# One job of fifteen block products in place of two jobs of seven, in a fused graph-attention kernel

## The chip, the cores and the metric

The kernel runs on one core of a Trainium2 chip. The metric is the device time in microseconds (us). A profiled execution gives, besides, a trace of every instruction. The engines are called as in the profile: PE (TensorE, matrix products), PEld (its weight loads), DVE (VectorE), ACT (ScalarE), POOL (GpSimd) and SP (the queue that issues the DMAs). Each engine works through its own instructions in the order in which the program lists them.

## The reference, cut to what matters

Two graph-attention layers, each with a residual and a layer norm, on x of 128 graphs x 64 nodes x 768 features, all in float32. The change lies wholly in layer 0, which has 12 heads of 64:

```python
h = jnp.einsum('bnd,ade->bane', feat_in, W)
th = jnp.tanh(h)
attn = (th . w_src) + swapaxes(th . w_dst)          # per head
attn = jnp.where(attn >= 0, attn, 0.2 * attn)
attn = softmax(jnp.where(~adj, -999.0, attn))
feat_out = elu(attn @ h + b)
gate = jax.nn.sigmoid(feat_in @ H_w.T + H_b)
x = layernorm(x + gate * feat_out + (1.0 - gate) * feat_in)
```

Layer 1 is a masked attention with 6 heads of 128 (q, k, v, output projection). It follows as a second stage and the change leaves its arithmetic alone.

## The kernel before, in words

The 8192 nodes are 32 pairs of two tiles; a tile is 128 nodes (two graphs), so a pair is 256 rows. Stage 1 runs layer 0 and the v projection of layer 1, pair by pair; stage 2 runs q, k, attention and the output projection of layer 1.

In stage 1, h = x W (768 x 768) and the gate logits = x H (768 x 768) are each a product of a pair's 256 x 768 rows with a 768 x 768 matrix. Each is computed as a 2 x 2 block product in seven products instead of eight (class Job, L247): the x blocks are 128 rows x 384, the weight blocks 384 x 384, and sums of blocks replace the eighth product. A product is three matmuls of 384 columns (L270), one for each 128 of the 384 that are summed over. Four sums of x blocks per pair are made on POOL (L240 to L243, `block_sums`), four sums of weight blocks once on DVE (L216 to L219). The results leave PSUM as copies on ACT (L850, L852) and as adds on DVE (L851 for h, L866 to L868 for the gate, where the first write also adds the bias). The v projection (`v_job`, L871) has the same form.

The order on each engine is written out by hand. A list gives the order of PE's products in a turn (TURN: h1, h2, u4, u3, h6, g1, h5, h7, g2, ..., where h and g are of the new pair p, v of the old pair q = p - 1, and u is the rest of the v job before that). After the product at each position of the list, the actions planned for that position are emitted (`at` for the new pair, `was` for the old one). A product's way out of PSUM is emitted one product later (`step`, L305). PSUM banks are shared out by tag (y, z: three each, m: two).

For each tile of the new pair the actions are, in this order: `products` (tanh of h on ACT, L888, then times w_dst on DVE, L889, and w_src on POOL, L890), `terms` (L893: the sums over each head on DVE, L897; these 12 numbers per node go out to DRAM, L899, and come back spread over all partitions, L902, as the tile dd), `logits` (dd plus the own term, DVE, L926), `leaky` (ACT, L936), `masked` (mask, maximum, subtraction: DVE, L942, L948, L949), `exps` (ACT, L955). In the turn after, the tile is old: `probs_by_nodes` (transposes on PE, L966, copies on ACT, L967), `gate_tanh` (ACT, L1067, L1068), `residual` (POOL, L1017), `attend` (48 small matmuls, L987), `features` (DVE, L1003, L1004, then exp on ACT, L1011), `elu1` and `gated` (DVE, L1022, L1027, L1029), `stats` and `normed` (DVE, POOL L322, ACT L327), `by_features` (transposes and copies), and then the v products and their block sums (`v_sums`, DVE). The two tiles of the new pair are called n1 and n0 (n1 goes first), those of the old pair t1 and t0.

In TURN `terms` of n1 and n0 stand at positions 13 and 14, `logits` at 16 and 18, `masked` at 18 and 20, so that DVE's list reads: sums over heads of n1, two gate adds, sums of n0, two v block sums and a v add, logits of n1, and so on. Of PE's list around the turn's start: h1, transposes, h2, u4, attend of t1, u3, transposes, h6; the product that needs h1's way out of PSUM (h6) stands after `attend`.

Stage 2 uses the same idea with 15 products of 256 x 256 blocks (WIDE, classes Wide and Out, L447 and L494).

## Time and profile before

| what | value |
|---|---|
| three runs | 2884.24, 2886.47, 2887.24 us (median 2886.47) |
| span of the profiled execution | 2888.2 us (the page gives no other time for it) |
| stage 1, to the first key product of stage 2 | 1525.6 us |
| time from pair to pair in stage 1 (e.g. `features` of t1, 700.96 to 746.53) | 45.57 us |
| mean of that over 28 pairs (h1 at 140.97 to h1 at 1423.92) | 45.8 us |
| in that stretch of 45.57 us, busy: PE, DVE, POOL, ACT | 44.99, 37.12, 21.38, 20.02 us |
| granted PE clock, mean | 0.998 |

The busy time of an engine is the time in which at least one of its instructions ran; an idle entry in brackets behind an instruction gives how long the engine stood before it and what ended that. The "critical chain" is followed back from the last instruction to what released it, step by step.

### The profile page before, as it was taken

What the parts mean: (1) busy time and instruction counts of PE and PEld (TensorE: products, weight loads), DVE (VectorE), ACT (ScalarE), POOL (GpSimd) and SP (SyncE); (2) the same over time, 40 slices, a digit from 0 to 9 for tenths busy, and PEclk for the clock granted to TensorE, in tenths of its full rate; (3) what the DMA queues carried; (4) which work ended last, traced back from release to release, by engine and by line L of the source; (5) the groups of instructions that cost most, each with busy time, mean ns of one, the idle gap of its engine ahead of it and who ended that gap; (6) DMA issues with size and microseconds to landing.
All of it is one profiled execution on the core that took longest, in us unless ns stands there. A gap on an engine that the chain in (4) does not pass through costs nothing.

```text
span 2888.2 us, 47874 instructions
## 1 busy us (share of the span) xinstructions
PE 2840.2 (98%) x18252; PEld 2075.9 (72%) x18252; DVE 1924.9 (67%) x3203; ACT 1061.2 (37%) x1896; POOL 1303.5 (45%) x1253
## 2 busy tenths in 40 slices
PE   8999999999999999999999999999999999999998
PEld 4565556666566666666668888888888888888886
DVE  7888888887888888777763545555544555554556
ACT  2444444444444444444433223333222333322332
POOL 3444445454444544343343445343545443444534
PEclk9999999999999999999999999999999999999999
DMA  5444444444445444333353434432323333233432
GB/s 182 132 154 145 140 150 143 159 148 151 141 142 162 135 155 142 105 116 108 121 195 96 122 91 111 111 92 84 77 79 111 111 104 95 68 84 94 111 88 74
DMA packets 322068, 348.73 MB, mean 121 GB/s; under 512 B 147888, under 2 KB 247216, under 8 KB 321840
## 3 DMA queue, kind: packets, MB, share of 16 engines
q1 hardware_dynamic: 321840, 345.66, 39.7%
q8 instruction: 146, 2.39, 0.4%
q14 instruction: 82, 0.67, 0.1%
HBM read 198.48 MB, written 122.29 MB: 111 GB/s over the span
## 4 chain that ended last, share of the span: by engine, by line
PE 80%; DVE 9%; DMA 4%; ACT 3%; issue 2%; POOL 1%; SPq 1%; POOLq 0%; DVEq 0%; ACTq 0%
PE z_k L447 9%; PE z_o L494 9%; PE z_q L447 8%; PE y_h L270 6%; PE y_g L270 6%; PE y_k L447 6%; PE y_o L494 6%; PE y_q L447 5%; PE y_v L270 5%; PE z_h L270 4%; PE z_v L270 3%; PE z_g L270 2%; PE cp L634 2%; PE sp L550 2%; PE x_g L270 2%
## 5 line engine op out<-in xcount | busy, mean ns | idle before, releaser
L574 ACT ACTIVATE sc<-sc 128x512 f32<-128x512 f32 x48 | 30.7, 639 | 616.9 <-DVE sc L571 616.9
L695 POOL TENSOR_TENSOR y<-y,bf_bc 128x768 f32<-128x768 f32 x64 | 114.7, 1817 | 295.1 <-DMA y<-x1d 265.5
L507 DVE TENSOR_TENSOR y<-y,z_o 128x256 f32<-128x256 f32 x320 | 127.4, 417 | 140.0 <-PE z_o L494 139.9
L494 PE MATMUL z_o<-wf,so 128*128 128x256 f32 x896 | 215.8, 383 | 2.3 <-DVE y L507 1.2
L447 PE MATMUL z_q<-xs,w_wq 128*128 128x256 f32 x896 | 213.5, 381 | 1.0 <-POOL xs L411 0.9
L411 POOL TENSOR_TENSOR so<-ctxT 128x256 f32<-128x256 f32 x224 | 160.5, 737 | 89.8 <-PE y_o L494 44.0
L447 PE MATMUL z_k<-xs,hw_wk 128*128 128x256 f32 x840 | 200.0, 381 | 0.0
L447 PEld LDWEIGHTS z_q<-xs,w_wq 128*128 128x128 f32 x896 | 168.7, 190 | 25.0 <-POOL xs L411 1.3
L494 PEld LDWEIGHTS z_o<-wf,so 128*128 128x128 f32 x896 | 167.2, 190 | 26.9 <-issue 2.0
L322 POOL TENSOR_TENSOR rs_b<-ve_b,minus_half 128x1 f32<-128x1 f32 x64 | 40.5, 632 | 312.7 <-DVE ve_b L320 311.9
L1017 POOL TENSOR_TENSOR x<-gate,x 128x768 f32<-128x768 f32 x64 | 120.1, 1878 | 135.1 <-ACT gate L1068 121.6
L890 POOL TENSOR_TENSOR th<-th,wsd 128x768 f32<-128x768 f32 x64 | 118.0, 1844 | 137.7 <-DVE th L889 137.7
L447 PEld LDWEIGHTS z_k<-xs,hw_wk 128*128 128x128 f32 x840 | 160.3, 191 | 22.1
L322 POOL TENSOR_TENSOR rs_a<-ve_a,minus_half 128x1 f32<-128x1 f32 x64 | 35.9, 562 | 307.3 <-DVE ve_a L320 307.3
L411 POOL TENSOR_TENSOR xs<-r,r 128x512 f32<-128x512 f32 x112 | 147.8, 1338 | 39.5 <-DMA r<-x1Td 22.5
L462 DVE TENSOR_TENSOR qT<-qT,z_q 128x512 f32<-128x512 f32 x96 | 65.9, 687 | 140.8 <-PE z_q L447 140.8
L270 PE MATMUL y_h<-w_wq,xT 128*128 128x384 f32 x384 | 136.5, 492 | 8.3 <-DMA w_wq<-in_w_dram 7.7
L462 DVE TENSOR_TENSOR kT<-kT,z_k 128x512 f32<-128x512 f32 x96 | 66.0, 687 | 114.9 <-PE z_k L447 112.9
L270 PE MATMUL z_v<-wv,sv_v 128*128 128x384 f32 x384 | 137.5, 494 | 1.0 <-DVE v L880 1.0
L270 PE MATMUL y_v<-wv,x1T 128*128 128x384 f32 x384 | 136.5, 492 | 1.2 <-ACT v L879 0.9
L270 PE MATMUL z_h<-w_wq,sx_x 128*128 128x384 f32 x384 | 137.5, 494 | 0.0
L270 PE MATMUL y_v<-wv,sv_v 128*128 128x384 f32 x384 | 134.9, 488 | 1.9 <-DVE sv_v L241 1.0
(165 smaller groups left out, 6907.7 us busy)
## 6 DMA issues: line engine op xcount, KB each, us to landing
x<-in_x_dram SPq DMA_DIRECT2D x64, 384.0 KB, 3.7
dd<-dstd SPq DMA_DIRECT2D x128, 192.0 KB, 3.4
x1d<-x SPq DMA_DIRECT2D x64, 384.0 KB, 2.6
x1Td<-x1T SPq DMA_DIRECT2D x32, 768.0 KB, 4.5
vd<-v SPq DMA_DIRECT2D x64, 384.0 KB, 2.9
r<-x1Td SPq DMA_DIRECT2D x96, 256.0 KB, 3.4
v<-vd SPq DMA_DIRECT2D x384, 64.0 KB, 2.3
y<-x1d SPq DMA_DIRECT2D x64, 384.0 KB, 5.7
```

Of the source, the lines that this page charges most:

```text
L270: T.matmul(to[:, : self.n], lhsT, rhs, start=kc == 0 and not more, stop=kc == HK - 1, skip_group_check=more,)
L322: G.tensor_tensor(rstd, ve, minus_half, ALU.pow)
L411: G.tensor_tensor(t, self.of(x[0]), self.of(x[2]), x[1])
L447: T.matmul(b[:, half * W2 : (half + 1) * W2], w[:, kc, half * P : (half + 1) * P], x[:, kc, :], start=half == kc == 0 and not more, stop=k ...
L462: V.tensor_tensor(at, at, b.rearrange("p (h t) -> p h t", h=2), ALU.add if sign > 0 else ALU.subtract,)
L494: T.matmul(b[:, :W2], x[:, kc, :], w[:, kc, :], start=kc == 0 and not more, stop=kc == 1, skip_group_check=more,)
L507: V.tensor_tensor(at, at, self.banks[path][:, :W2], ALU.add if sign > 0 else ALU.subtract)
L550: T.matmul(self.sp_[gr * N : (gr + 1) * N, (i * 2 + a) * N : (i * 2 + a + 1) * N], qT[:, 2 * self.f + a, at], kT[:, 2 * self.f + a, at], s ...
L634: T.matmul(self.cp_[a][e, at], self.v_[rows, i, gr, e], self.scT_[rows, at], start=True, stop=True,)
L695: G.tensor_tensor(y, y, pools["bf"], ALU.add)
L890: G.tensor_tensor(th[:, 1, :], th[:, 1, :], wsd[:, 1, :], ALU.mult)
L1017: G.tensor_tensor(xp, st[t]["gate"], xp, ALU.mult)
```

## The change

- h and gate become one product: the 256 x 768 rows times one 768 x 1536 matrix (W and H side by side). It is cut 3 x 2 x 3: x blocks of 128 rows x 256, weight blocks of 256 x 512, in 15 products (PRODUCTS) instead of 18. Each product is two matmuls of 512 columns. The products run in the order ORDER, adding up in five paths; a path is one PSUM bank, and a product that adds to a path waits until the path's earlier readers have read.
- The weight blocks: nine are loaded, 17 sums (128 x 1024 numbers each) are made once on DVE (`made`) and one negation on ACT. Ten sums of x blocks per pair (128 x 256) on POOL take the place of four (128 x 384).
- Way out of PSUM per pair: six copies on ACT and ten adds on DVE, each 128 x 512, where there were four copies on ACT and ten operations on DVE, each 128 x 384. The gate's bias is added by POOL (`gate_bias`, two per pair, 128 x 768). h and gate of a tile lie in one tile hg, four of them in rotation.
- The turn's list becomes a0 a5 a3 a1 a8 a6 a7 a2 a10 a9 a12 a4 a14 a11 v1 v2 v6 v5 v7 a13 v4 v3; all seven v products are of the old pair. The actions move with it (below). For the first three pairs one stream of 45 products runs, with v of pairs 0 and 1 put in near its end.
- The weights of q and k of stage 2 go into the room of the new weight tile, in the order in which the last pair sets it free.

```diff
+PRODUCTS = [
+    (0, (2, 0), [(2, 0, -1)]),
+    (3, (1, 1), [(0, 1, -1)]),
...
+    (0, (2, ALU.add, (0, 0)), [(2, 1, -1)]),
...
+    (4, ((0, 1), ALU.subtract, 3), [(0, 1, 1), (1, 1, 1)]),
...
+ORDER = (0, 5, 3, 1, 8, 6, 7, 2, 10, 9, 12, 4, 14, 11, 13)
...
+HEAD = [f"a{n}" for n in ORDER[:14]]
+TURN = HEAD + ["v1", "v2", "v6", "v5", "v7", "a13", "v4", "v3"]
...
+        def negated():
+            S.mul(wa[:, 0], wa[:, 14], -1.0)
+
+        def made(i):
+            dst, a, op, b = MADE[i]
+            V.tensor_tensor(wa[:, dst], wa[:, a], wa[:, b], op)
...
+        class Fifteen:
...
+            def product(self, n):
+                path = PRODUCTS[n][0]
+                more = path in self.banks
+                if not more:
+                    tag = "y" if path in (0, 2) else "z"
+                    self.banks[path] = bank(tag, f"{tag}_a{self.p}_{n}", 3)
+                b, x = self.banks[path], A[self.p][n]
+                for kc in range(2):
+                    T.matmul(
+                        b,
+                        x[:, kc, :],
+                        wa[:, n, kc, :],
...
+            def way_out(self, n):
+                path, _, reads = PRODUCTS[n]
+                b = as_heads(self.banks[path])
+                for f, t, sign in reads:
...
+                    if (f, t) in self.written:
+                        V.tensor_tensor(at, at, b, ALU.add if sign > 0 else ALU.subtract)
+                    elif sign > 0:
+                        S.copy(at, b)
+                    else:
+                        S.mul(at, b, -1.0)
...
+        def gate_bias(t):
+            gt = gate_of(t)
+            G.tensor_tensor(gt, gt, as_heads(hb_bc), ALU.add)
...
+        stream = [(p, f"a{n}") for p in range(3) for n in ORDER]
...
+        for q, a0, a1 in ((0, 0, 36), (1, 37, 3 * NW - 1)):
+            items += stream[a0:a1] + values[q][:5] + stream[a1 : a1 + 1] + values[q][5:]
...
+                was(0, do(probs_by_nodes, t1), do(exps, t0), do(gate_tanh, t1))
+                was(1, do(residual, t1))
+                was(2, do(attend, t1), do(gate_tanh, t0))
+                was(3, do(features, t1), do(probs_by_nodes, t0), do(residual, t0))
...
+                was(11, do(v_begins, q), do(v_sum, q, 0), do(by_features, t0))
+                was(14, do(v_sum, q, 1), do(spill_features, q))
+                was(15, do(v_sum, q, 2))
+                was(17, do(v_sum, q, 3))
...
-            at(11, new, do(products, n1))
...
-            at(12, new, do(products, n0))
-            at(13, new, do(terms, n1), do(with_bias, n1))
-            at(14, new, do(terms, n0), do(with_bias, n0))
...
-            at(16, new, do(logits, n1))
-            at(17, new, do(leaky, n1))
...
-            at(18, new, do(masked, n1), do(logits, n0))
-            at(19, new, do(exps, n1), do(leaky, n0))
-            at(20, new, do(masked, n0))
+            at(7, do(products, n1))
+            at(8 if p != 1 else 15, do(inputs, p))
+            at(9, do(terms, n1), do(with_bias, n1))
+            at(12, do(logits, n1))
+            at(13, do(leaky, n1), do(products, n0))
+            at(14, do(masked, n1))
+            at(14 if p != 1 else 17, do(plus_one, p))
+            at(15, do(exps, n1), do(terms, n0), do(with_bias, n0), do(gate_bias, n0))
+            late = p == NP - 1
+            at(18 - late, do(logits, n0))
+            at(19 - late, do(leaky, n0))
+            at(20 - late, do(masked, n0))
+            at(21 if p < NP - 1 else 17, do(gate_bias, n1))
```

As the built program has it, DVE's list of a turn in the steady part becomes: features of t1; add of a1; elu1 and gated of t1; add of a8; stats of t1; add of a6; features of t0; mask; add of a7; elu1 and gated of t0; times w_dst of n1; stats of t0; add of a10; sums over heads of n1; add of a12; v block sum 1; add of a4; logits of n1; add of a14; times w_dst of n0; add of a11; v block sum 2; masked of n1; v block sum 3; sums over heads of n0; a v add; v block sum 4; logits of n0; a v add; add of a13; masked of n0; a v add. On ACT the negated copy of a0 stands behind exps of t0 and gate_tanh of t1; on PE, a3 (same path as a0) stands ahead of attend of t1.

## The prediction

> **What bounds the kernel now.** I read the page's busy times first, then PE's waits by stretch, then the critical chain and DVE's and PE's timelines of one pair.

> ```profile
> PE 2840.2 (98%) x18252; PEld 2075.9 (72%) x18252; DVE 1924.9 (67%) x3203; ACT 1061.2 (37%) x1896; POOL 1303.5 (45%) x1253
> ```

> PE is busy 98%; in the waits view it loses only 6.2 us between 200 and 1350 us. So stage 1 goes at PE's pace: 14 h and gate products, 7 of v, four sets of transposes and two `attend` per pair.

> ```profile
> 736.26 2.10 PE L270 MATMUL y_v<-wv,sv_v 128*128 128x384 f32 x6
> 738.20 2.10 PE L270 MATMUL y_h<-w_wq,xT 128*128 128x384 f32 x6
> ```

> Starts are 1.94 us apart (the 2.10 overlaps the next). 21 x 1.94 + 4 x 0.66 + 2 x 0.86 + 0.4 us of handing over = 45.5; one pair measured 45.57. But a second loop is almost as long. The critical chain, 724 to 747 us:

> ```profile
> 724.82 1.95 PE y_v L270 x6
> 726.77 0.36 SPq L902
> 727.17 3.83 DMA dd<-dstd
> 731.10 1.53 DVE att L926
> ...
> 743.20 0.84 ACT prob L955
> 744.04 0.74 ACT gate L1067
> 744.81 0.84 ACT gate L1068
> 745.65 0.38 ACT h L850
> 746.06 0.56 DVE h L851
> ```

> It leaves PE for a trip through DRAM (dd), goes through DVE and ACT, and returns to `features`. DVE's timeline of the same stretch:

> ```profile
> 723.38 1.74 DVE L897 TENSOR_REDUCE sd<-th 128x24 f32<-128x1536 f32 x1
> 725.04 0.54 DVE L866 TENSOR_TENSOR gate<-y_g,hb_bc 128x384 f32<-128x384 f32 x1
> ...
> 726.09 1.74 DVE L897 TENSOR_REDUCE sd<-th 128x24 f32<-128x1536 f32 x1
> 727.75 1.77 DVE L241 TENSOR_TENSOR sv_v<-sv_v,x1T 128x384 f32<-128x384 f32 x1
> ...
> 731.10 1.52 DVE L926 TENSOR_TENSOR att<-dd,sd 128x768 f32<-128x768 f32 x1 [0.65 <-DMA dd<-dstd]
> ```

> The sums over heads of n1 end at 725.12, dd is there at 731.10: the trip takes 6.0 us. DVE fills it with the gate adds, the sums of n0 and v block sums, and waits 0.65 us. This filling is what the change takes away.

> [...] at 746.06 DVE's add of h waits 2.47 us for ACT, and `features` behind it waits too. [...] Here six passes took 4.21 us, not 1.94, shortly after an idle stretch of 3.31 us:

> ```profile
> 82.86 1.54 PE L966 MATMUL x1Tp<-ident,x 128*128 128x128 f32 x6 [3.31 <-ACT x L327]
> 84.69 4.21 PE L270 MATMUL y_v<-wv,x1T 128*128 128x384 f32 x6 [0.29 <-ACT x1T L967]
> ```

> [...] Here L1022 takes 0.96 us alone and 1.35 to 1.85 beside POOL, while adds from PSUM keep their 0.55.

> **PE's part.** No 128x512 matmul is in stage 1, but a stage 2 product streams the same 2048 columns (8 passes of 256; the new one 4 of 512) and takes 1.73 us in the chain. 15 x 1.73 = 25.95 against 14 x 1.94 = 27.16: 1.2 us less, PE's pace 44.3 us per pair. With fewer, longer passes it may be 1.71 (0.3 us more gained). This counts only if PE stays the bound.

> **DVE's part.** Ten operations of 0.55 go; ten of 128x512 come. That shape from PSUM is on the page:

> ```profile
> L462 DVE TENSOR_TENSOR qT<-qT,z_q 128x512 f32<-128x512 f32 x96 | 65.9, 687 | 140.8 <-PE z_q L447 140.8
> ```

> 0.69 us each, in sequence about 0.6 (0.46 for the 0.55 one): +1.4 us per pair on 37.1. That alone would fit. The order does not. I add up the new loop from the start of `features` t1, in DVE's order, with spacings from 700.96 to 746.53:
> - features 1.4; add 0.6; wait for exp 0.4; elu1 and gated of t1 3.9 (as beside POOL before); add 0.6; stats 1.4; add 0.6; features t0 1.4; mask 0.3; add 0.6; elu1 and gated t0 3.1; w_dst of n1 1.0; stats 1.4; add 0.6; shift 0.5 (POOL's power now queues behind its 1.8 us multiply); sums of n1 1.7. Sum 19.5.
> - dd of n1: 6.0, now covered by only an add, a v sum and an add (1.7): DVE stands 4.3. Behind this wait are queued the adds of a14 and a11 and all of n0. At 25.5.
> - logits n1 1.5; ACT's leaky n1 and tanh n0 0.85 each plus 0.1; w_dst of n0 1.0; add 0.6; v sum 1.5; masked n1 3.1; v sum 0.6; sums of n0 1.7. At 37.3.
> - dd of n0: 6.0, covered by a v add and a v sum (1.0): DVE stands 5.0. At 43.3.
> - logits n0 1.5, two adds 1.1, masked 3.1. At 49.0.
> - ACT: exp 0.84, tanh and subtraction 0.75 each, then the negated copy of a0, about 0.65 (a 128x512 ACT operation on SBUF, L574, takes 0.639): 3.1 with handing over. a3 must wait for that copy (same bank), and `attend` stands behind a3: 1.73 + 0.95 + 0.15. In the order before, `attend` had no such wait. At 54.9.
> - 0.6 more for POOL in the way of L926, L949, L889 (means 1.78, 1.14, 1.18 against 1.52, 0.96, 0.96 alone).

> Sum 55.5 us per pair, bounded by 52.5 (dd 5.0 twice, no contention) and 58.5 (a late SP, more contention). Before: 45.8 on average. So +9.7 over 28 turns: +272 us. In the last turn no a3 stands ahead of `attend`: +2.

> **The rest of the change.** POOL: ten sums at 0.74 (L411, 128x256) are 7.4 for 5.2 (1.52, 1.39, 1.20, 1.13), and two gate biases at 1.8: +5.8 on 21.4, half the new period; hidden in waits, except as contention above. ACT: six copies at 0.6 for four at 0.47, +1.7 on 20.0; only the one behind `gate_tanh` counts. SP: per tile the same dstd, dd and hx issues, those of n1 and n0 now apart; the x1d store of t0 stands ahead of dstd of n1, its source ready about 0.5 us before the sums end. If it is later, the first dd slips by as much: in the upper bound. `attend` streams 65 columns for 66: nothing. The weights of q and k: same bytes, loaded while the last pair runs; if that cover failed a few us, not more.

> **Start.** Until `features` of turn 3 (149.24 us before), DVE gets nine more weight sums (17 x 1.2 for 8 x 1.35, L216's shape: +10 us) and three pairs' adds; I count about 130 us of DVE work, 8 us to the first data, and 28 us of the same waits for dd and ACT: 166. PE alone would reach that point 14 us earlier than before. I take +15, range -14 to +25.

> **Sum.** 2888.2 (the span of the profiled execution) + 272 + 2 + 15 = 3177; the median of the runs is 1.7 lower: 3175. Stage 2 is untouched.

> **Rivals.**
> - PE stays the bound (the other side). Mechanism: fewer columns, 1.2 us per pair, decisive as long as DVE's loop is under 45.8 us: 28 x 1.5 (45.8 to 44.3) and 14 at the start, 2886 - 42 - 14 = 2830. For it: PE's 98% and DVE's average of 81%. Against: 38.5 us of DVE work and 9.3 of forced waits for dd are already 47.8.
> - Only the dd waits bite; the wait of a3 is hidden because ACT gets to the copy in time. Loop 55.5 - 5.4 = 50.1: 28 x 4.3 + 8: 3015. For it: slack elsewhere. Against: the copy stands behind exp of n0 in ACT's list.
> - PE gets cold as well: it now idles some 2 to 3 us three times a turn. At half clock a3 and `attend` cost 2.7 more: 58.2, 28 x 12.4 + 20: 3253. Against: no single idle stretch is clearly over the 3.3 us seen.
> - The change does nothing (the gains and waits cancel): 2886.

> **How the numbers follow.** DVE loop as summed 0.62 (3080 to 3270 by its bounds); cold PE 0.15; dd alone 0.12; PE bound 0.08; no change 0.03. The range 3010 to 3270 leaves out the last two, and part of the second and third. About 0.2% is what a measurement of this kernel can tell from no change: faster 0.08, same 0.03, slower 0.89.

> **What would show it.** After: PE busy near 80% (44.3 of 55.5) in stage 1, waiting at a3 for ACT; DVE idle at logits in every turn, 4 and 5 us, put down to dd; DVE waiting for PE at `features`; the distance from one `features` of t1 to the next near 55 us; 4 passes of a product in 1.73 us; stage 2 as before. The forecast is wrong if DVE's wait at logits is under 2 us, or if dd arrives within 3 us of the sums.

## The result, and the profile after

| | before | after |
|---|---|---|
| median of four runs | 2885.35 us | 3316.17 us |
| lowest and highest | 2880.94, 2887.24 | 3310.73, 3324.14 |
| span of the profiled execution | 2888.2 us | 3322.4 us |
| granted PE clock, mean | 0.998 | 0.96 |

After over before is 1.1497 (95% interval 1.1478 to 1.1516): the change makes the kernel 15% slower. The forecast had the direction and the kind of cause. It had the size too small: 3175 us, with 3270 as its upper end.

The span of the profiled execution grew by 434.2 us. Here it is split by the starts of `features`, that is of the first reciprocal (L1003 before, L1045 after) of each t1:

| stretch | before | after | difference | forecast |
|---|---|---|---|---|
| start, to `features` of turn 3 | 149.2 | 189.0 | +39.7 | +15 |
| 28 turns, mean of one | 45.79 | 59.73 | +13.94, times 28: +390.2 | +9.7, times 28: +272 |
| from there to the first key product of stage 2 | 94.1 | 101.9 | +7.8 | +2 |
| stage 2, from that product on | 1362.7 | 1359.1 | -3.6 | 0 |

The first line of the page that answers to the one shown of before (engine, busy us, share, instructions):

```profile
PE 2932.8 (88%) x17484; PEld 1967.4 (59%) x17484; DVE 1982.4 (60%) x3218; ACT 1090.1 (33%) x1961; POOL 1509.8 (45%) x1503
```

No engine is busy throughout any more: PE fell from 98% to 88% of a longer span, and DVE from 67% to 60%. So the time has to be sought in waits that run through several engines. The page's group of the logits says where to look first (busy us, mean ns of one, then the idle time ahead of the group and what ended it):

```profile
L968 DVE TENSOR_TENSOR att<-dd,sd 128x768 f32<-128x768 f32 x64 | 97.5, 1523 | 283.4 <-DMA dd<-dstd 283.4
```

DVE stood 283 us in front of its 64 logits. The critical chain of one turn, 705 to 728 us (start, length, what), tells what that wait delays:

```profile
705.72 1.66 DMA dstd<-sd
...
707.97 3.91 DMA dd<-dstd
712.06 1.34 issue
713.40 0.56 DVE v L922
714.00 4.21 PE z_v L273 x6
718.21 2.66 PE y_a L890 x4
721.98 0.86 ACT prob L997
722.83 0.74 ACT hg L1115
723.60 0.84 ACT hg L1116
724.44 0.50 ACT hg L910
724.98 1.98 PE y_a L890 x4
726.96 0.86 PE av L1029 x48
```

The forecast had the chain's first part (dd, the logits) and its end (ACT's exp, tanh, subtraction, negated copy, a3, `attend`). It had nothing of the middle: after the logits of n0 DVE makes the z-add of v7 (L922). The product v3 writes to the bank that this add reads, so v3 waits on PE, and a0, the transposes behind a0 and ACT's copies of them are late with it. Over the 28 turns v3 waits 3.3 us on average. PE's timeline of these microseconds (the brackets give PE's idle time and what ended it):

```profile
708.48 2.10 PE L273 MATMUL y_v<-wv,x1T 128*128 128x384 f32 x6
714.00 4.21 PE L273 MATMUL z_v<-wv,sv_v 128*128 128x384 f32 x6 [3.43 <-DVE v L922]
718.01 2.86 PE L890 MATMUL y_a<-wa,sx 128*128 128x512 f32 x4
720.70 0.82 PE L1008 MATMUL pTp<-ident,prob 128*128 128x128 f32 x6
...
724.98 1.98 PE L890 MATMUL y_a<-wa,sx 128*128 128x512 f32 x4 [1.74 <-ACT hg L910]
```

v3 takes 4.21 us where the product above it takes 2.10, and a0 2.86 where four passes (one product) take 1.88 elsewhere: after 3.43 us of idleness PE ran at half clock (the granted clock from 714.0 to 718.2 us was 0.50). DVE's timeline and then ACT's show what a late a0 does:

```profile
716.56 0.96 DVE L991 TENSOR_TENSOR att<-att,mx 128x768 f32<-128x768 f32 x1
```

```profile
721.23 0.86 ACT L1009 COPY pT<-pTp 128x384 f32<-128x384 f32 x2 [6.50 <-PE pTp L1008]
721.98 0.86 ACT L997 ACTIVATE prob<-att 128x768 f32<-128x768 f32 x1
```

The exp of n0 (prob) had its input at 717.5 us, when the masked step ended. It stands in ACT's list behind the copies of the transposes of t1, which wait 6.50 us for PE. So it starts 4.5 us after its input was there, and all that follows it in the chain is late by as much. Over the 28 turns this delay is 3.2 us on average (1.3 to 4.6).

PE has three more waits in a turn (means of the 28): 3.5 us ahead of v6, for the second v block sum, which stands in DVE's list behind the logits of n1; 2.2 us ahead of a12, for an add on DVE; 1.8 us at a3.

That PE's new products are as quick as forecast is seen in the starts of two neighbours, 1.71 us apart:

```profile
736.44 1.88 PE L890 MATMUL z_a<-wa,sx 128*128 128x512 f32 x4
738.15 1.88 PE L890 MATMUL y_a<-wa,sx 128*128 128x512 f32 x4
```

### The profile page after: what moved, and what is told of

The parts are those of the page before. It is cut to its first block, busy times and chain, and to the rows that moved or that the text cites. A ratio compares the mean times of both kernels' runs of the same rounds, so it can differ in the third digit from the quotient of the medians.

```text
span 3322.4 us, 46633 instructions
## 1 busy us (share of the span) xinstructions
PE 2932.8 (88%) x17484; PEld 1967.4 (59%) x17484; DVE 1982.4 (60%) x3218; ACT 1090.1 (33%) x1961; POOL 1509.8 (45%) x1503
## 4 chain that ended last, share of the span: by engine, by line
PE 52%; DVE 23%; DMA 10%; issue 6%; ACT 5%; POOL 2%; SPq 1%; DVEq 0%; POOLq 0%; ACTq 0%
PE z_o L501 7%; PE z_q L454 7%; PE z_k L454 7%; DMA dd<-dstd 7%; PE y_o L501 5%; PE y_k L454 5%; PE y_q L454 5%; PE y_a L890 5%; PE z_v L273 3%; DMA dstd<-sd 3%; DVE hg L906 3%; DVE sd L939 2%; PE z_a L890 2%; DVE ex L1070 2%; DVE ex L1064 2%
## 5 line engine op out<-in xcount | busy, mean ns | idle before, releaser
L890 PE MATMUL y_a<-wa,sx 128*128 128x512 f32 x1024 | 518.6, 637 | 154.5 <-DVE hg L906 79.9
L890 PEld LDWEIGHTS y_a<-wa,sx 128*128 128x128 f32 x1024 | 200.7, 206 | 404.7 <-issue 199.5
L968 DVE TENSOR_TENSOR att<-dd,sd 128x768 f32<-128x768 f32 x64 | 97.5, 1523 | 283.4 <-DMA dd<-dstd 283.4
L454 PE MATMUL z_q<-xs,wa 128*128 128x256 f32 x896 | 213.2, 381 | 0.0
L454 PE MATMUL z_k<-xs,wa 128*128 128x256 f32 x840 | 198.5, 379 | 0.0
L273 PEld LDWEIGHTS z_v<-wv,sv_v 128*128 128x128 f32 x384 | 91.0, 244 | 176.4 <-DVE v L922 112.3
L1059 POOL TENSOR_TENSOR x<-hg,x 128x768 f32<-128x768 f32 x64 | 107.5, 1680 | 187.0 <-ACT hg L1116 184.2
L890 PE MATMUL z_a<-wa,xT 128*128 128x512 f32 x384 | 190.0, 618 | 0.0
L454 PEld LDWEIGHTS z_q<-xs,wa 128*128 128x128 f32 x896 | 168.8, 190 | 23.4
L1045 DVE RECIPROCAL rden<-av 128x6 f32<-128x6 f32 x128 | 24.1, 188 | 249.8 <-PE av L1029 249.8
L454 PEld LDWEIGHTS z_k<-xs,wa 128*128 128x128 f32 x840 | 159.5, 190 | 21.7
```

The costliest lines, as they stand in the source:

```text
L273: T.matmul(to[:, : self.n], lhsT, rhs, start=kc == 0 and not more, stop=kc == HK - 1, skip_group_check=more,)
L454: T.matmul(b[:, half * W2 : (half + 1) * W2], w[:, kc, half * P : (half + 1) * P], x[:, kc, :], start=half == kc == 0 and not more, stop=k ...
L890: T.matmul(b, x[:, kc, :], wa[:, n, kc, :], start=kc == 0 and not more, stop=kc == 1, skip_group_check=more,)
L968: V.tensor_tensor(att3, dd.rearrange("p (m a) -> p a m", a=H0), sd[:, H0:].unsqueeze(2).to_broadcast([P, H0, N]), ALU.add,)
L1059: G.tensor_tensor(xp, gate_of(t), xp, ALU.mult)
```

## The experiments

The theory: the time is lost to the order of DVE's list (logits that wait for dd, with the z-add of v7 behind them), closed to a loop by ACT's order, and PE's cold clock adds to it. The rivals, as the expectations number them: (1) the 15 products are slower in themselves; (2) ACT's chain behind the masked step alone sets the end; (3) the clock is the main cost; (4) POOL is the bound. The edits are to the changed kernel, most of them to its schedule lines and in the 28 turns of pairs 3 to 30 (two of the expectations say 27). "Turn" is the mean distance between the `features` of t1, as in the table.

### adds_first: DVE's adds ahead of the wait

```diff
+mid = 3 <= p < NP - 1
-at(18 - late, do(logits, n0))
-at(19 - late, do(leaky, n0))
-at(20 - late, do(masked, n0))
+at(20 if mid else 18 - late, do(logits, n0))
+at(20 if mid else 19 - late, do(leaky, n0))
+at(21 if mid else 20 - late, do(masked, n0))
```

> 28 turns are changed: the logits of n0 go behind DVE's adds of v7 and a13, the masked step behind v4. Theory 1 (DVE's order closes the loop: z-add of v7 stands behind the wait for dd, so v3, a0, the transposes and ACT's copies are late): DVE does 1.7 us of adds inside the 5.4 us wait, and v3 no longer waits for DVE, so PE stays warm there; 4 to 5.5 us less per turn, 3316 - 28 x 4.75 = about 3185 (3160 to 3205). Rival 2 (the ACT chain after the masked step alone sets the end): the adds were not on it; within 20 us of 3316. Rival 3 (PE's clock is the main cost): the clock returns to 0.99 and the time falls by more than 6 us per turn, under 3150.

Measured: 3281.4 us, turn 58.31. Only 1.4 us of the 4.75 came. PE's timeline tells why:

```profile
702.88 2.10 PE L273 MATMUL z_v<-wv,sv_v 128*128 128x384 f32 x6
...
713.22 3.78 PE L890 MATMUL y_a<-wa,sx 128*128 128x512 f32 x4 [4.15 <-ACT hg L910]
```

v3 does not wait any more and is warm (2.10 us), as the theory said. But now a3 waits 4.15 us and is cold (3.78 us for four passes): the masked step of n0 comes later, and ACT's exp, tanh and negated copy still stand behind it. Over the 28 turns v3's wait of 3.3 us is gone, and a3's has grown from 1.8 to 4.5 us. One wait was exchanged for the next on the same loop.

### copy_first: ACT's negated copy ahead of exp and tanh

```diff
-was(0, do(probs_by_nodes, t1), do(exps, t0), do(gate_tanh, t1))
-was(1, do(residual, t1))
+was(0, do(probs_by_nodes, t1))
+was(1, do(exps, t0), do(gate_tanh, t1), do(residual, t1))
```

> ACT's exp of n0 and tanh of n1's gate go one product later, behind the negated copy of a0, in every turn. Theory 1: the copy no longer stands behind exp and tanh (0.84 + 0.75 + 0.9 us), but a0 is late anyway because v3 is, and then attend of n1 comes earlier while exp of n0 comes later: 1 to 2 us less per turn, 3260 to 3290. Rival 2 (this ACT chain sets the end): 2.5 to 4 us less per turn, 3205 to 3245. If exp of n0 is on the path instead, slower than 3316.

Measured: 3281.7 us, turn 58.47, in the range of theory 1. It is the mirror image: a3 does not wait, and v3 still does, cold (3.4 us on average):

```profile
757.00 4.21 PE L273 MATMUL z_v<-wv,sv_v 128*128 128x384 f32 x6 [3.15 <-DVE v L922]
```

### old_dd and no_dd: the trip taken out of the wait

```diff
-in_=dst_d[t][g * N : (g + 1) * N, :]
+in_=dst_d[max(t - 2, t % 2)][g * N : (g + 1) * N, :]
```

> dd is read from what the pair before wrote, so that the transfer waits for nothing of this pair (the logits are computed from the wrong destination terms; all other work is the same). The wait for dd should vanish from DVE's list. Theory 1: at least the 9.8 us of waits per turn go, and with them the wait of v3 and the cold clock: 9 to 13 us less per turn, 2950 to 3065, and PE the bound again if over 13. Rival 2: dd's wait is hidden, within 20 us of 3316. Rival 4 (POOL's contention and the longer DVE and POOL work set the turn): 0 to 3 us per turn, over 3230.

Measured: old_dd 3227.5 us, turn 56.46. It missed, since the edit did less than was meant: in SP's list the load of dd still stood behind the store of the sums, so dd was waited for 3.4 us each time. So the trip was taken out altogether:

```diff
-dd.rearrange("p (m a) -> p a m", a=H0),
+wsd[:, 0, :].rearrange("p (m a) -> p a m", a=H0),
```

> The logits read a fixed tile of the same shape (wsd) in place of dd, so nobody waits for the trip through DRAM; the transfers themselves stay, and the destination terms are wrong. In the run that read dd from the pair before, dd was still waited for (3.4 us each time in place of 4.7, as its issue stands behind the store of the sums on SP's queue), and 2.6 us less of waits per turn gave 3.2 us less time. Theory 1: the same exchange goes on, 9.4 us of waits times 1.2 is 11 us per turn, 2980 to 3050. Rival 2 (masked step, ACT and a3 set the turn whatever dd does): it stops at about 3220. Rival 4 (POOL's queue is the next bound): 3100 to 3180.

Measured: no_dd 3108.7 us, turn 52.82: 6.9 us less per turn, for 9.4 us of waits. Rival 2 falls (it stopped at 3220). The time is above the range of theory 1 and in that of rival 4, POOL's queue as the next bound. The trace agrees in part: v3's wait is down to 0.2 us, and the loop closes through a3 once more, in ACT's timeline by way of POOL's gate bias (L1110):

```profile
760.28 0.84 ACT L1115 ACTIVATE hg<-hg 128x768 f32<-128x768 f32 x1 [2.73 <-POOL hg L1110]
...
761.91 0.58 ACT L910 ACTIVATE hg<-y_a 128x512 f32<-128x512 f32 x1
```

and a3 waits 4.58 us there. The turns in which POOL makes weight sums of stage 2 take 53.4 us, the seven after them 51.0: these sums are some 2.5 us of what is left, not all of it. In the start, `features` of turn 3 come at 172.8 us in place of 189.0: the waits for dd are 16 of the 40 us lost in the start.

### both_sums and three_edits: the order of before for the sums

```diff
-at(12, do(logits, n1))
-at(13, do(leaky, n1), do(products, n0))
-at(14, do(masked, n1))
+both = 3 <= p < NP - 1
+at(13, do(products, n0))
+at(16 if both else 12, do(logits, n1))
+at(16 if both else 13, do(leaky, n1))
+at(17 if both else 14, do(masked, n1))
...
-at(15, do(exps, n1), do(terms, n0), do(with_bias, n0), do(gate_bias, n0))
+at(15, do(terms, n0), do(with_bias, n0), do(gate_bias, n0))
+at(18 if both else 15, do(exps, n1))
```

> The logits and masked step of n1 go behind the sums of n0 (as in the kernel before), so that both trips of dd lie beside DVE work; 28 turns. Theory 1: the wait of n1 goes (4.4 us), that of n0 falls from 5.4 to about 1 because logits and masked of n1 (4.6 us) lie in it; 7 to 9 us less per turn, 3065 to 3120. Rival 2: the masked step of n0 ends the turn as before, no change over 20 us. Rival 4: 0 to 3 us per turn.

Measured: 3158.6 us, turn 53.88: 5.9 us less per turn, the largest gain of a single move in the order. Both trips of dd now lie beside DVE's work: DVE waits 0.2 us per turn for them where it waited 9.2 (means of 28 turns). It is short of the 7 to 9 us expected because new waits came up: DVE waits for POOL (4.67 us at the sums of n0 at 757.6 us; 1.6 us per turn on average), and v7 for ACT's copy of v6, which stands behind the leaky step of n1 (3.1 us per turn).

> The edits of both_sums, adds_first and copy_first together. If they take away different waits, the gains add: 3316 - 158 - 35 - 35 = about 3090. If they take away the same one (in both_sums DVE waits only 1.4 us for dd of n0, and v3 only 0.3 us for DVE): 3140 to 3160. If ACT's exp of n0, now later, holds the transposes: over 3160.

Measured: 3147.2 us, turn 53.57. The gains of the three edits do not add. They take waits off one loop, and the next one of it, v7 behind ACT's list (3.36 us in the turn seen), was there already. adds_first and copy_first were not run together without both_sums, so what these two give alone is not shown.

### kept_warm: the cost of the cold clock

```diff
+def warm(p, i):
+    b = bank("m", f"warm_{p}_{i}")
+    for _ in range(4):
+        T.matmul(b[:, :HALF], ident, wv_w[:, B11, 0, :], start=True, stop=True)
...
+if 3 <= p < NP - 1:
+    at(15, do(warm, p, 0))
+    at(20, do(warm, p, 1))
```

> The changed kernel with eight idle products per turn in 27 turns (four 128x384 products of constant data into a spare bank ahead of v6, four ahead of v3, 2.6 us each time), which lie inside PE's two waits of 3.4 to 3.9 us[...]. Nothing else is changed; PE's busy time without them is 2933 us, against 2841 us in own_order for the same products, so cold products cost 91 us in all, 3.3 per turn. If the cold clock is on the path (rival 3, as an addition to theory 1): 2 to 3.3 us less per turn, 3225 to 3265. If it only fills time in which PE would wait anyway: within 15 us of 3316. If the added products come in the way: slower.

Measured: 3262.0 us, turn 57.70. Adding eight matmuls per turn makes the kernel 54 us faster, 2.0 us per turn. v3 on PE's timeline:

```profile
753.92 2.74 PE L1147 MATMUL warm<-wv,ident 128*128 128x384 f32 x8
757.28 2.20 PE L273 MATMUL z_v<-wv,sv_v 128*128 128x384 f32 x6 [0.61 <-DVE v L922]
```

2.20 us in place of 4.21. So the cold clock is a real part: 2.0 of 13.9 us. That is a lower bound, since some cold products are left (the granted clock is 0.982; 0.960 in the changed kernel, 0.998 in the kernel before). The cold products of the changed kernel cost PE 91 us in all, by the expectation's count, of the 431: as a direct cost the clock is not the main one, and rival 3 falls.

### own_order: an order laid out for the new products

The order was worked out from the durations in the trace so that each product's bank is free in time at PE's own pace. Its core:

```diff
+was(0, *[do(masked, t0)] * (q > 2), do(gate_tanh, t1))
+was(1, do(probs_by_nodes, t1), do(residual, t1))
+was(2, do(exps, t0), do(attend, t1), *[do(gate_tanh, t0)] * (q == 2), do(residual, t0))
...
+was(9, do(gated, t0))
+was(10, do(stats, t0))
+was(11, do(normed, t0))
+was(12, do(v_begins, q), do(v_sum, q, 0), do(by_features, t0))
...
+at(11, do(terms, n1), do(with_bias, n1))
+at(13, do(products, n0))
...
+at(15, do(terms, n0), do(with_bias, n0), do(gate_bias, n0))
+at(16, do(logits, n1))
+at(17, do(leaky, n1))
+at(18, do(masked, n1))
+at(19, do(gate_tanh, n0))
+at(20, do(exps, n1), do(gate_bias, n1))
+at(21, do(logits, n0), do(leaky, n0))
```

> A new order of 27 turns, laid out so that PE never waits at its own pace: both sums before both logits, the sums of n1 after the adds that free a12, the masked step of n0 in the next turn after v3's add, gate_tanh of n0 at the end of its own turn, exp of n0 behind the negated copy of a0. Theory 1 (the order, not the form of the products, costs the time): PE's pace of 44.3 to 46 us per turn, the start still 40 us late: 2870 to 2930. If POOL's queue (weight sums of stage 2 that wait for their loads, with th and pow behind them) is the next bound, 48 to 50 us per turn: 2970 to 3050. If the 15-product form itself is slower (rival 1): no better than three_edits, over 3080.

Measured: 3019.6 us, turn 48.94. With the same instructions in another order, 297 us of the 431 are back. It is the POOL case of the expectation. The last six turns before the last pair, in which POOL has no weight sums of stage 2 left, take 45.8 or 45.9 us each; with them a turn is 47.2 to 55.6. POOL's timeline of a turn with them, and then DVE's:

```profile
708.22 0.73 POOL L369 TENSOR_TENSOR wacc_k<-wacc_k,wadd_k 128x256 f32<-128x256 f32 x1 [2.82 <-DMA wadd_k<-in_wk_dram]
...
712.18 1.81 POOL L932 TENSOR_TENSOR th<-th,wsd 128x768 f32<-128x768 f32 x1
```

```profile
714.02 1.75 DVE L939 TENSOR_REDUCE sd<-th 128x24 f32<-128x1536 f32 x1 [3.19 <-POOL th L932]
```

POOL waits for a weight load, the multiplication th is behind it in POOL's list, and DVE waits for th. In the changed kernel this costs next to nothing: its turns take 59.8 us with the weight sums and 59.5 in the seven turns after they end. So rival 4 falls for the changed kernel; POOL's queue came to set the turn only when the larger waits were gone.

### order_2, early_loads, order_3, order_3_start: four further orders, all slower than own_order

The edits of order_2, on top of own_order:

```diff
-was(10, do(stats, t0))
-was(11, do(normed, t0))
-was(12, do(v_begins, q), do(v_sum, q, 0), do(by_features, t0))
+was(11, do(stats, t0), do(normed, t0))
+was(12, do(v_begins, q), do(v_sum, q, 0))
+was(13, do(by_features, t0))
...
-for _ in range(1 + i % 2):
+for _ in range(2 * (not 8 <= (i - new_at[3]) % LONG <= 13)):
...
-at(18, do(masked, n1))
-at(19, do(gate_tanh, n0))
-at(20, do(exps, n1), do(gate_bias, n1))
-at(21, do(logits, n0), do(leaky, n0))
+at(18, do(logits, n0))
+at(19, do(leaky, n0), do(masked, n1), do(gate_tanh, n0))
+at(20, do(gate_bias, n1))
+at(21, do(exps, n1))
```

> own_order with five more moves: the add of a12 ahead of the statistics of t0, the z-add of v7 ahead of the masked step of n1, the logits of n0 ahead of it too, the loads of x behind the first dd on SP, and POOL's weight sums of stage 2 and sums of x kept out of the products 8 to 13, where th is multiplied. In own_order a turn takes 48.9 us on average and 45.9 in the last turns, in which no weight sums of stage 2 are left. Theory 1 with POOL as the next bound: 45 to 47 us per turn, 2890 to 2965. If POOL's waits for the loads only move elsewhere: 48 to 50, 2990 to 3040.

Measured: 3134.9 us, turn 52.95, against every expectation. Yet this miss shows the mechanism once more, for it puts the logits of n0 ahead of the z-add of v7 again. DVE's timeline, then PE's:

```profile
754.83 1.49 DVE L968 TENSOR_TENSOR att<-dd,sd 128x768 f32<-128x768 f32 x1 [5.52 <-DMA dd<-dstd]
756.24 0.55 DVE L922 TENSOR_TENSOR v<-z_v,v 128x384 f32<-128x384 f32 x1
```

```profile
756.84 4.21 PE L273 MATMUL z_v<-wv,sv_v 128*128 128x384 f32 x6 [4.10 <-DVE v L922]
```

It is the picture of the changed kernel: DVE waits for dd, then the z-add, then v3, late and cold (six passes in 4.21 us, as in the changed kernel at a granted clock of 0.50).

early_loads, on top of order_2:

```diff
+                        yield
                         yield
                         yield
                         yield
                         G.tensor_tensor(acc, acc, t, ALU.add if sign > 0 else ALU.subtract)
```

> order_2, with each load of a weight block for POOL's sums issued one step (half a product or one) earlier, so that POOL waits less for it with th and the bias adds behind it. If these waits are what the 3 us between 48.9 and 45.9 consist of: 1 to 2 us less per turn than order_2. [...]

Measured: 3108.8 us, turn 52.08. 0.9 us per turn from one step's more lead, just under the 1 to 2 expected.

order_3 puts order_2's tail (its last four lines) back as in own_order, and:

```diff
-for _ in range(2 * (not 8 <= (i - new_at[3]) % LONG <= 13)):
+for _ in range(2 * (not 8 <= (i - new_at[3]) % LONG <= 15)):
```

> order_2 with its tail put back as in own_order: the masked step of n1 at v7, the logits of n0 only after the add of a13 (order_2 had them ahead of the z-add of v7, and DVE stood there 5.5 us for dd while v3 waited, cold). POOL's weight sums are kept out of the products 8 to 15, so that no load of theirs stands ahead of the store of n0's sums on SP's queue. Theory 1 (one wait for dd ahead of the z-add of v7 is what made order_2 slow): back under own_order's 48.9 us per turn, 45 to 47: 2890 to 2965. If the five moves at the front are what made order_2 slow: over 3020.

Measured: 3087.3 us (ratio to before 1.0704, 1.068 to 1.0728), turn 51.36. This missed also. v3's wait is gone (0.4 us per turn in place of 3.7), but only 1.6 of the 4.0 us per turn that order_2 had lost came back. The weight sums, pressed into fewer places, now stand ahead of the gate bias on POOL; ACT's tanh waits 4.78 us for that bias, and a3 3.71 us for ACT. Its last three turns, without weight sums, take 47.1 or 47.2 us, not 45.9, so the moves at the front were no gain either.

order_3_start moves the logits of the first three pairs:

```diff
+at(12 if late else 14, do(logits, n1))
+at(13 if late else 14, do(leaky, n1))
+at(14 if late else 15, do(masked, n1))
...
+at(17 if late else 20, do(logits, n0))
+at(18 if late else 20, do(leaky, n0))
+at(19 if late else 21, do(masked, n0))
```

> order_3 with the same change for the first three pairs: the logits of n1 two products later, those of n0 two products later and the masked step behind another. In no_dd the features of turn 3 came 16 us earlier than in the changed kernel (172.8 against 189.0 us), so the waits for dd are 16 of the 40 us that the start lost. If later logits fill them: 8 to 14 us less than order_3. If the start is bound by DVE's weight sums and the first products: within 4 us of order_3.

Measured: 3073.9 us (1.0649, 1.063 to 1.0667). `features` of turn 3 come at 177.2 us, 10.2 earlier than in order_3: as expected.

### own_start, quiet_pool, fewer_sums: what was left

own_start is own_order with the edits of order_3_start and of early_loads, shown above.

> own_order with the later logits of the first three pairs (as in order_3_start) and with each weight load for POOL's sums of stage 2 issued one step earlier. The start: the later logits took 13 us off order_3, so 8 to 13 us here. The loads: if POOL's waits for them (5.5 us in a turn seen, with th and the bias adds behind them) are the difference between 48.9 and 45.9 us per turn, 1 to 2 us per turn more: 2955 to 2985. If only the start gains: 3005 to 3012.

Measured: 2969.7 us (1.0295, 1.0278 to 1.0313), turn 47.50, `features` of turn 3 at 176.7: both gains came. It is the best order found with the new products, and it is 2.95% slower than the kernel before.

quiet_pool is own_order with one line out:

```diff
-G.tensor_tensor(acc, acc, t, ALU.add if sign > 0 else ALU.subtract)
```

> own_order without POOL's additions of weight blocks for stage 2 (the loads and stores stay; stage 2 gets unsummed weights). In own_order a turn is 45.9 us where these sums have ended and 49.5 where they run. If they are what stands between the two: all turns at 45.5 to 46.5, 22 turns x 3.5 us, 2930 to 2950. If the turns at the end are short for another reason: 2990 to 3020. Either way this says how far the new products come in a good order: the kernel before needs 45.8 us per turn.

Measured: 2944.1 us, turn 46.36, most turns 45.8 or 45.9: POOL's weight sums are 2.6 of the 3.0 us between 48.9 and 45.9. The sums over 700 to 1400 us of this kernel (length, PE, PEld, DVE, ACT and POOL busy, PE clock) show PE 97% busy at full clock:

```profile
700.00:1400.00 700.00, 676.09 (x3350) 348.78 (x3349) 605.43 (x822) 324.20 (x516) 388.55 (x335) 1.00 0.43 135
```

In a turn of 45.8 us PE still waits 1.3 us, mostly for the add of a12. That leaves 44.6 us of work, where the forecast had 44.3 as PE's pace. Rival 1 falls: the 15 products are not slower. But what they can save against the 45.8 us of a turn before, 1.2 us, is all that there was to win per turn, and even this order does not bring it in.

fewer_sums is the changed kernel with:

```diff
 for n in ns:
-    at(pos, do(made, n))
+    if n not in (2, 4, 5, 6, 8, 10, 11, 12, 13):
+        at(pos, do(made, n))
```

> The changed kernel without nine of the sums of weight blocks that DVE makes in the start (wrong weights; as many sums are left as the kernel before makes). If the start (features of turn 3 at 189.0 us in place of 149.2) is bound by DVE's work: 9 x 1.2 = 11 us earlier, about 178, and 3305. If it is bound by the waits for dd and by PE's waits alone: within 3 us of 189.

Measured: 3307.6 us, `features` of turn 3 at 181.5 us: 7.5 us of the start go with DVE's nine extra weight sums, between the two expectations.

## Why the prediction was right or wrong, point by point

- **PE's part: right.** 1.73 us per product forecast, 1.71 to 1.72 measured; pace 44.3 forecast, 44.6 found once the order let PE run.
- **DVE's part: right.** The new add takes 0.68 us, spaced by 0.60; 0.69 and 0.6 were forecast.
- **The waits for dd: right.** 4.3 us for n1 and 5.0 for n0 forecast, 4.3 and 4.9 measured as means of the 28 turns (4.20 and 5.38 in the turn from 667.3 to 727.9).
- **The sum of the turn: one term failed.** By its own terms, forecast and measured (means of the 28 turns, from DVE's timeline): `features` to the sums of n1 19.5 and 19.0; dd of n1 6.0 and 6.8; on to the sums of n0 11.8 and 13.0; dd of n0 6.0 and 5.9; logits, adds and masked step of n0 5.7 and 5.8; from there to `features` 5.9 and 9.2. (0.6 more was forecast for POOL in DVE's way, without a place.) So 3.3 of the 4.2 us that the turn takes over the forecast lie in the last term. It is the step "ACT: exp 0.84, tanh and subtraction 0.75 each, then the negated copy of a0 ... a3 ... `attend`". Its length was right: from the start of the exp of n0 to `features` it takes 5.9 us. But it took ACT to be free when the masked step ended, and the exp starts 3.2 us later. "logits n0 1.5, two adds 1.1" was written one line earlier; the question who waits for these two adds was not asked. v3 does, a0 stands behind v3, the transposes of t1 behind a0, ACT's copies behind these, and the exp behind the copies. The runs take this chain apart at both ends: adds_first frees v3, and a3 waits; copy_first frees a3, and v3 waits.
- **The cold clock: the argument against it was wrong.** It was kept as a rival at 58.2 us per turn because "no single idle stretch is clearly over the 3.3 us seen". v3 and v6 wait 3.3 and 3.5 us on average, up to 4.0 and 6.5, and then take 3.7 and 3.1 us on average where 2.1 is full speed (2.10 us at a granted clock of 1.00, at 704.83 us). It is no rival but an addition: at least 2.0 us per turn by kept_warm. The forecast had put PE's idle stretches at 2 to 3 us; these two are longer. v3 at 714.00 us ran at a granted clock of 0.50 after 3.43 us of idleness, and in adds_first four passes took 3.53 us, where 1.88 is full speed, after only 1.91 us (below). That shorter stretches would leave the clock alone was the author's estimate, from the one stretch of 3.31 us in the trace of before; it was not shown.
- **The start: mis-sized.** DVE's work was forecast as 130 us to `features` of turn 3, and its busy time to 189.0 us is 132.1. DVE's first data came at 7.5 us (8 forecast). The term that failed is "28 us of the same waits": 189.0 less 132.1 less 7.5 is 49. 16 us of the start go with dd, 7.5 with the extra weight sums; the two were not taken away together, so they may overlap. If they do not, about 16 us of the 40 stay open; if they do, more.
- **The last turn and stage 2.** +7.8 us in place of +2: the turn after the 28 takes 61.2 us where it took 51.6, and why stays open. Stage 2 as forecast, -3.6 in 1363.
- **The range.** Its upper bound of 58.5 us per turn was made of longer trips and more contention. It held no term for a wait that the forecast had not seen.

## What to carry to other kernels

When an action that waits is moved on one engine, go through what stands behind it in that engine's list, and for each item ask which product, copy or DMA waits for it on another engine: a loop through the lists of three engines can hold up a product that never waits for the transfer itself, as v3 here. Take a wait away and the next one of the loop takes its place, so single edits give less than their waits (6.9 us for 9.4 of dd), while an order worked out as a whole gave 10.8 us per turn with the same instructions. Before such work is begun, price what the change can bring at best: here 1.2 us in 45.8 per turn.

## What the runs showed of the hardware

```profile
731.03 1.88 PE L890 MATMUL y_a<-wa,sx 128*128 128x512 f32 x4
734.82 3.53 PE L890 MATMUL y_a<-wa,sx 128*128 128x512 f32 x4 [1.91 <-DVE hg L906]
```

After 1.91 us of idleness four passes took 3.53 us, and the granted clock from 735 to 740 us was 0.66. In the 28 turns of adds_first PE waits 1.9 to 2.1 us ahead of this product, a12, each time: in 11 of them it then takes 2.8 to 3.6 us, in 17 it is at full speed (the product at 731.03 us took 1.88 us at a granted clock of 1.00). In copy_first it took 1.95 us after 2.38 us of idleness in one turn. So the length of a single stretch does not tell whether the clock falls. What else decides it, no run here shows.
